# Placing TensorE's side products in the attention layer of a four-layer convolution kernel

## The chip, the core and the metric

The kernel runs on one core of a Trainium2 chip. The metric is the device time of one execution, in microseconds. Three runs of the kernel before took 3672.72, 3662.45 and 3675.35 us; their median is 3672.72 us.

## What is computed

The input x has 4 images of 256 channels and 48 x 48 pixels. Four layers run one after the other, each of the form x = x + layer(group norm of x). The first three are convolutions. The change lies in the fourth, a linear attention over square windows:

```python
q = sigmoid(einsum('bchw,oc->bohw', x, Wq)).reshape(b * h, d, Hh, Ww)
k = sigmoid(einsum('bchw,oc->bohw', x, Wk)).reshape(b * h, d, Hh, Ww)
v = einsum('bchw,oc->bohw', x, Wv).reshape(b * h, d, Hh, Ww)
v = v / maximum(norm(v, axis=1, keepdims=True), 1e-12)
for w in (1, 2, 4):                       # windows of 48, 24 and 12 pixels
    wk = box(integral(k), Hh // w)        # sum of k over the window
    wkv = box(integral(k outer v), Hh // w)
    attn = einsum('bdhw,bdfhw->bfhw', q, wkv)
    norm = einsum('bdhw,bdhw->bhw', q, wk)
    outs.append((attn / (norm[:, None] + 1e-06)).reshape(b, C, Hh, Ww))
return einsum('bchw,oc->bohw', concatenate(outs, axis=1), Wout) + bout
```

There are h = 8 heads of d = 32 channels. All data are float32.

## The kernel before

**Layers 0 to 2** fill the first 1388 us or so. The projections of the first image to q, k and v are begun there too.

**Layer 3** works image by image (b, 4 of them), channel half by channel half (ct, 2 halves of 4 heads) and row block by row block (rb, 6 blocks of 8 rows): 48 *blocks* in this order (`order`, before the main loop). Instead of integral images, the kernel computes for each block the scores q times k against *tiles* of keys (8 rows a by 16 columns c), multiplies them with a 0/1 mask for each of the three windows, and multiplies the masked scores with v. A block has 12, 15 or 18 tiles (`tiles_of`, line 1913), 720 tiles in all. Tiles that the smallest window sees ("near") alternate with those that it does not see ("far" in the code) as long as there are both. For key rows that the largest window sees whole, the middle part of its product comes from a ready sum (`window_state`, `whole`), and only strips of columns need the mask.

**One step of the main loop** (it runs over `stream`, defined at line 2069) issues, for tile n:

- `scores` (line 1763): 4 score products s of 32 rows on TensorE, one for each head, into two PSUM buffers of two heads each (pool ps_s);
- `masked` (line 1781): VectorE multiplies s with the masks of the largest window and, for near tiles, of the middle window, into sm; ScalarE copies s to sm where the tile has only the middle window's part left; GpSimd multiplies sm with the mask that remains;
- the `sums` (line 1890) of tile n - LAG, with LAG = 2: products of sm and v, into three accumulators acc, 4 heads side by side;
- `advance()` (line 237), which lets every *side job* go on.

Every engine runs what it is given in this order (`InOrder`, line 135, keeps the program's order). A product that stands in TensorE's queue before the next scores is therefore paid before them.

**Side jobs** are generators. Each `yield n` puts a job to sleep for n steps. `advance()` counts the step and lets the jobs that are due issue what comes next. The jobs with products on TensorE are:

- `qk` and `v` (lines 338 and 373): the projections of the next image, 2 products of 384 columns or 2 of 256 columns into proj_ps;
- `state` (line 1672): transposes of the keys (keys_ps) and products of keys and v (kv_ps) for the ready sums;
- `norms` (line 1577): the denominators. GpSimd subtracts and multiplies box sums (nhi, nlo, nq) in two halves of channels, and TensorE sums over the channels of each head (norm_ps): 3 products for each half, side by side in the array, each of 384 columns;
- `finish` (line 1960): when a block of the second half ct = 1 is done, VectorE multiplies its sums (stage) with reciprocal denominators (rc), one window at a time (`dve.tensor_mul(stage...)`). Then two output products (mo = 0, 1), each an accumulation of 6 products of 384 columns (out_ps <- o and stage in turn), are added to x and stored. o holds the sums of the first half's heads, which went through HBM.

All these use one PSUM bank (pool ps_m, tag st). `bank(steps)` (line 261) waits until the bank is free, and marks it taken for so many steps. It knows nothing of what TensorE has to do:

```python
def bank(steps):
    nonlocal bank_free
    while step < bank_free:
        yield 1
    bank_free = step + steps
```

`prepare` (line 1927) loads o, the residual res and 8 pieces of rc for a block of the second half, in the middle of this block, and lets GpSimd multiply o with its rc. `take("o")` waits for a free o buffer, of which there is one; `finish` gives it back at its end. There are two buffers each of rc and res.

`until(keys)` (line 252) calls `advance()` until something is made that the main loop needs, without a tile in between: what is pending is then issued in one go. At the end of the kernel `while active: advance()` does the same with what is left.

Of the kernel before, what the change touches and what calls it, by code (L numbers as in the profile page):

```python
# [81 lines left out]

LAG = 2
ATTN_EPS = 1e-6


MROWS = [2 * h + RB - 1 for h in HALVES]
MCOL0 = [max(h, KC) for h in HALVES]
# [6 lines left out]
def window_masks():  # L95

    ki, kj = np.divmod(np.arange(P), KC)
    ms = []  # L100
    for h, nr, m0, ncol in zip(HALVES, MROWS, MCOL0, MCOLS):
        qi = np.arange(nr) - h + 1
# [44 lines left out]
def conv_preact_kernel(  # L147
# [84 lines left out]

    step, bank_free = 0, 0
    made = set()
    active = []

    def advance():

        nonlocal step
        step += 1  # L240
        for entry in list(active):
            if entry[0] <= step:
                wait = next(entry[1], None)
                if wait is None:
                    active.remove(entry)
                else:
                    entry[0] = step + wait
# [12 lines left out]

    def bank(steps):

        nonlocal bank_free
        while step < bank_free:
            yield 1
        bank_free = step + steps


    free = {"xr": 2, "xn": 2, "kt": 2, "sq": 2, "vt": 1, "cs": 1, "o": 1, "rc": 2, "res": 2}

# [17 lines left out]
    class Projection:  # L288
# [49 lines left out]
        def qk(self, g, a, name, mo):  # L338
# [5 lines left out]
            yield from take("kt")  # L344
            yield from bank(1)
            ps = self.ps_tile()[:, 0:NB]
# [26 lines left out]
        def v(self, g, a, c):  # L373
# [11 lines left out]
            vt, ss = self.vs[g]  # L385
            yield from bank(1)
            ps = self.ps_tile()[:, 0:C].rearrange("p (h d) -> p h d", d=D)
# [1095 lines left out]
    with (  # L1483
# [93 lines left out]
        def norms(b, rb):  # L1577
# [51 lines left out]
            yield 1  # L1629
            yield from bank(1)  # L1630
            ps = ps_m.tile([P, 512], F32, tag="st", name="norm_ps")
            for ct in range(NCT):
                for wi in range(NW):
                    pe.matmul(
                        ps[D * wi : D * (wi + 1), 0:NB],
                        head_sel[:, ct, :],
                        sums[ct][:, wi].rearrange("p r w -> p (r w)"),
                        start=(ct == 0),
                        stop=(ct == NCT - 1),
                    )  # L1640
            yield 1
            ns = scr.tile([D * NW, NB], F32, tag="ns", name="ns", bufs=1)
# [29 lines left out]
        def state(b, ct, a):  # L1672
# [3 lines left out]
            yield FETCH  # L1676
            yield from bank(2)
            ps = ps_m.tile([P, 512], F32, tag="st", name="keys_ps")[:, 0 : NKC * P]
# [60 lines left out]
        def rows_whole(a, rb):  # L1739

            return abs(a - rb) * RB + RB <= HALVES[0]
# [10 lines left out]
        class Block:  # L1752
# [28 lines left out]
            def masked(self, a, c, ss):  # L1781
# [145 lines left out]
        def prepare(i):  # L1927
# [32 lines left out]
        def finish(i, stage):  # L1960
# [11 lines left out]
            os = (o, stage)  # L1972
            for wi in range(NW):
                dve.tensor_mul(stage[:, wi], stage[:, wi], rc[:, wi])
                yield 1
            free["rc"] += 1
            for mo in range(NCT):
                yield from bank(2)
# [79 lines left out]
        def done(i):  # L2058
# [13 lines left out]
            for n, (a, c) in enumerate(tiles_of(rb))  # L2072
        ]
        blocks, ahead = {}, []
        start(window_state(0))
        start(finish_all())
        for n in range(len(stream) + LAG):
# [8 lines left out]
            if n >= LAG:  # L2086
# [12 lines left out]
                if last:  # L2099
                    done(i)  # L2100
            advance()
        while active:
# [45 lines left out]
```

## Time and profile before

| what | value |
|---|---|
| median of 3 runs | 3672.72 us |
| time of the profiled execution | 3665.04 us |
| span in its profile | 3663.2 us |
| mean granted TensorE clock | 0.952 |
| first score product of layer 3 | 1388.1 us |
| TensorE busy from 1388 to 3660 us | 2054.9 of 2272 us |
| VectorE busy there | 1494.5 us |
| GpSimd busy there | 1506.5 us |
| ScalarE busy there | 401.1 us |

The span runs from the first to the last instruction. The profile page gives each engine's busy time, a row of 40 slices of the span, the chain of work that ended last, and groups of instructions by operation and tile (out<-in) with the mean time of one and the idle time of the engine before them. A line of the waits view names the engine and operation that waited, what it waited for, the sum, the count and the longest. A line of the timeline has the start, the length, the engine, the operation, the tiles and the count, and in brackets the idle time before it and what ended it. PE is TensorE, PEld its weight load, DVE VectorE, ACT ScalarE, POOL GpSimd, SPq the queue of SyncE that issues DMAs. A product in float32 shows as two records.

### The profile page before, as it was taken

Reading aid. Unit: us, or ns where it says so; the run is one execution under the profiler, and the core shown is the slowest. Engines: PE = TensorE matmul, PEld = TensorE weight load, DVE = VectorE, ACT = ScalarE, POOL = GpSimd, SP = SyncE. Lnnn points to the kernel's source line nnn. Section 1 sums busy time; section 2 is a strip of 40 time slices with the busy share of each in tenths; the row PEclk is TensorE's granted clock in tenths of the full one; section 3 lists DMA queues with packets and bytes.
Section 4 is the critical chain, followed back from the end, with each engine's and each line's share of the span. In section 5 each row is a group of like instructions: output and inputs, shape, how many; then the busy total and the mean of one; then the engine's idle time right before and its main releaser. Section 6 shows DMA issues by size and latency. Waiting matters only on the chain. (4 is left out here: it accounts for less than half of the span.)

```text
span 3663.2 us, 73044 instructions
## 1 busy us (share of the span) xinstructions
PE 3216.3 (88%) x28754; PEld 1942.3 (53%) x28754; DVE 2419.0 (66%) x4987; ACT 677.5 (18%) x1557; POOL 1661.6 (45%) x2548
## 2 busy tenths in 40 slices
PE   3689998998997887887899889899998899999998
PEld 2467686786785664443444444444444444444444
DVE  7976587487484365876756576765577656566664
ACT  0012111111114422222101222211222201111100
POOL 0000120030030034787876786776476777454552
PEclk9789999999998898999999999999999999999999
DMA  7746324324314423344533543344223344211222
GB/s 252 227 139 197 105 94 129 112 85 127 102 65 138 136 72 108 122 141 144 149 103 112 157 122 122 108 126 137 81 96 120 119 128 129 64 32 32 66 62 61
DMA packets 373031, 423.29 MB, mean 116 GB/s; under 512 B 129075, under 2 KB 328531, under 8 KB 371539
## 3 DMA queue, kind: packets, MB, share of 16 engines
q1 hardware_dynamic: 371491, 416.32, 36.9%
q8 instruction: 229, 3.75, 0.4%
q0 software_dynamic: 144, 1.52, 0.2%
q14 instruction: 111, 0.91, 0.1%
q10 hardware_dynamic: 1056, 0.79, 0.1%
HBM read 288.79 MB, written 131.25 MB: 115 GB/s over the span
## 5 line engine op out<-in xcount | busy, mean ns | idle before, releaser
L143 DVE TENSOR_TENSOR sm<-s,masks 128x128 f32<-128x128 f32 (+8 forms) x2592 | 1145.8, 496 | 709.7 <-PE s L143 377.7
L143 POOL TENSOR_TENSOR sm<-sm,masks 128x432 f32<-128x432 f32 (+14 forms) x1152 | 822.9, 728 | 711.3 <-DVE sm L143 512.6
L143 PE MATMUL s<-qs,ks 32*128 32x320 f32 (+3 forms) x5760 | 870.4, 505 | 109.4 <-DVE sm L143 72.5
L143 PE MATMUL acc<-sm,vs 128*32 128x64 f32 (+13 forms) x14976 | 683.0, 308 | 32.2 <-POOL sm L143 32.1
L143 PE MATMUL cv<-vx,wt 128*128 128x288 f32 x2080 | 556.9, 423 | 92.3 <-DVE vx L143 49.5
L143 PEld LDWEIGHTS s<-qs,ks 32*128 32x128 f32 x5760 | 353.1, 188 | 479.8 <-issue 195.8
L143 PEld LDWEIGHTS acc<-sm,vs 128*32 128x32 f32 x14976 | 351.0, 111 | 441.6 <-issue 269.4
L143 PEld LDWEIGHTS cv<-vx,wt 128*128 128x128 f32 x2080 | 400.5, 197 | 212.6 <-issue 55.0
L143 POOL MEMSET v<- 128x16 f32 (+1 forms) x120 | 18.6, 215 | 722.4 <-DVE vx L143 628.3
L143 ACT COPY sm<-s 128x234 f32<-128x234 f32 (+5 forms) x384 | 123.4, 343 | 915.8 <-PE s L143 784.4
L143 PE MATMUL cv<-v,wl 128*128 128x384 f32 x1152 | 224.3, 354 | 22.4 <-DVE x L143 8.6
L143 PEld LDWEIGHTS cv<-v,wl 128*128 128x128 f32 x1152 | 214.6, 195 | 32.2 <-issue 15.2
L143 POOL TENSOR_TENSOR pt<-pt 128x144 f32<-128x144 f32 x336 | 185.3, 552 | 23.4 <-DVE pt L143 0.5
L143 POOL TENSOR_TENSOR v<-l2v,v 128x384 fp32r<-128x384 f32 x96 | 109.0, 1165 | 127.4 <-ACT v L143 118.7
L143 POOL TENSOR_TENSOR nhi<-nhi,nq 128x384 f32<-128x384 f32 x144 | 144.9, 1034 | 0.3
L143 PE MATMUL cv<-pad,wl 128*128 128x384 bf16 x864 | 143.1, 327 | 0.0
L143 PE MATMUL out_ps<-o,wout_sb 128*128 128x384 f32 x288 | 124.2, 514 | 12.3 <-DMA rc<-r_d 7.6
L143 ACT COPY stage<-acc 128x384 f32<-128x384 f32 x144 | 64.0, 489 | 303.7 <-PE acc L143 272.7
L143 PE MATMUL out_ps<-stage,wout_sb 128*128 128x384 f32 x288 | 118.4, 493 | 0.7 <-DVE stage L143 0.7
L143 DVE TENSOR_TENSOR vx<-v 128x868 f32<-128x868 f32 x112 | 115.3, 1055 | 0.5
L143 PEld LDWEIGHTS <-wl 128*128 128x128 bf16 x864 | 83.9, 97 | 59.4 <-issue 0.8
L143 DVE SCALAR_TENSOR_TENSOR x<-cv,alpha,x 128x384 f32<-128x384 f32 x144 | 83.9, 610 | 41.7 <-PE cv L143 41.4
(174 smaller groups left out, 3347.4 us busy)
## 6 DMA issues: line engine op xcount, KB each, us to landing
wt<-wt SPq DMA_DIRECT2D x48, 768.0 KB
kb_d<-pt SPq DMA_DIRECT2D x48, 576.0 KB
rc<-r_d SPq DMA_DIRECT2D x192, 144.0 KB
nhi<-kb_d SPq DMA_DIRECT2D x120, 192.0 KB
nlo<-kb_d SPq DMA_DIRECT2D x88, 192.0 KB
o_d<-stage SPq DMA_DIRECT2D x24, 576.0 KB
o<-o_d SPq DMA_DIRECT2D x24, 576.0 KB
wl<-wl_d SPq DMA_DIRECT2D x16, 768.0 KB
```

Of the source, the lines that this page charges most:

```text
L143: return lambda *args, **kwargs: self.tc.keep_in_program_order(op(*args, **kwargs))
```

## The change

- **An account of room.** `advance` gets a time for the step: 150 ns plus the VectorE time of the tile's masks (`mask_time`) less TensorE's time for the sums of the tile two steps before (`sums_time`), but at least 150 ns. The variable `spare` carries debts from step to step, but no savings. A side product is issued only when `spare` is at least 0.6 of its cost, and the cost is taken off. Costs count 1.67 ns for a column. In `until`, at the end and in the layers before, `advance()` has no time, and room is unlimited.
- **Output products in three pieces** of 2 products each, one for each window, each of which waits for room (`turn`). The bank is held (`HOLD`) until the last piece. In the first output product, the multiplication of stage for a window stands right before its piece, with one step between them; before, the three multiplications came first, a step apart.
- **Norms in two pieces**, one for each half of the channels.
- **Two buffers of o** in place of one, for the sums of the first half's heads. To make space, the mask of the largest window keeps only the rows that are used (23 in place of 55), and `times_mask` picks among them.

The products, the masks' values and what each engine computes stay the same.

```diff
-MROWS = [2 * h + RB - 1 for h in HALVES]
+MROWS = [3 * RB - 1 if h == H // 2 else 2 * h + RB - 1 for h in HALVES]
...
-    def advance():
+    def advance(time=None):
-        nonlocal step
+        nonlocal step, spare
         step += 1
+        spare = ALL if time is None else min(spare, 0.0) + time
...
+    ALL = 1e6
+
+    def turn(cost):
+        nonlocal spare
+        while spare < 0.6 * cost:
+            yield 1
+        spare -= cost
+
-    def bank(steps):
-        nonlocal bank_free
-        while step < bank_free:
+    def bank(steps, cost):
+        nonlocal bank_free, spare
+        while step < bank_free or spare < 0.6 * cost:
             yield 1
         bank_free = step + steps
+        spare -= cost
+
+    def keep_bank(steps):
+        nonlocal bank_free
+        bank_free = step + steps
+
+    def product_time(columns):
+        return 1.67 * columns
...
-    free = {"xr": 2, "xn": 2, "kt": 2, "sq": 2, "vt": 1, "cs": 1, "o": 1, "rc": 2, "res": 2}
+    free = {"xr": 2, "xn": 2, "kt": 2, "sq": 2, "vt": 1, "cs": 1, "o": 2, "rc": 2, "res": 2}
...
-            yield from bank(1)
+            yield from bank(1, NCT * product_time(NB))      # qk; v alike with C
...
-            yield from bank(1)
+            yield from bank(HOLD, 2 * product_time(NB))
             ps = ps_m.tile([P, 512], F32, tag="st", name="norm_ps")
             for ct in range(NCT):
+                if ct > 0:
+                    yield 1
+                    yield from turn(2 * product_time(NB))
...
+            keep_bank(1)
...
-            yield from bank(2)
+            yield from bank(2, product_time(NKC * P))       # keys and kv in state
...
+                    if wi == 0:
+                        mr = RB - 1 if full else 0 if a > rb else 2 * RB - 1
...
-            o = op.tile([P, NW, NB], F32, tag="o", name="o", bufs=1)
+            o = op.tile([P, NW, NB], F32, tag="o", name="o")
...
-            for wi in range(NW):
-                dve.tensor_mul(stage[:, wi], stage[:, wi], rc[:, wi])
-                yield 1
-            free["rc"] += 1
             for mo in range(NCT):
-                yield from bank(2)
+                yield from bank(HOLD, NCT * product_time(NB))
                 ps = ps_m.tile([P, 512], F32, tag="st", name="out_ps")[:, 0:NB]
                 for kt in range(NW * NCT):
+                    if kt % NCT == 0:
+                        if kt > 0:
+                            yield 1
+                            yield from turn(NCT * product_time(NB))
+                        if mo == 0:
+                            wi = kt // NCT
+                            dve.tensor_mul(stage[:, wi], stage[:, wi], rc[:, wi])
+                            yield 1
                     pe.matmul(
...
+                keep_bank(2)
+                if mo == 0:
+                    free["rc"] += 1
...
+        def mask_time(i, a, c):
+            rb = order[i][2]
+            def product(wi, cols):
+                y0, y1 = rows_seen(wi, a, rb)
+                return 2 * (2 * (y1 - y0) * (cols[1] - cols[0]) + 130) / 0.96
+            if not rows_whole(a, rb):
+                return product(0, cols_seen(0, c))
+            time = sum(product(0, cols) for cols in strips(c))
+            if seen(NW - 1, a, rb):
+                return time + product(1, cols_seen(1, c))
+            return time + 300
...
+            time = 1000.0
+            if LAG <= n < len(stream):
+                time = 150.0 + mask_time(*stream[n][:3]) - sums_time(*stream[n - LAG][:4])
+            advance(max(time, 150.0))
```

`sums_time` adds 1.67 ns for each column of the tile's sum products in each window that sees it, 300 ns for the first tile of a block and the time of the ready sums' products in the seventh.

More of the change, by code (lines that the diff above doesn't have):

```diff
@@ L83 @@
 LAG = 2
+HOLD = 1000
 ATTN_EPS = 1e-6
-MROWS = [2 * h + RB - 1 for h in HALVES]
+MROWS = [3 * RB - 1 if h == H // 2 else 2 * h + RB - 1 for h in HALVES]
 MCOL0 = [max(h, KC) for h in HALVES]
@@ L101, in window_masks @@
     for h, nr, m0, ncol in zip(HALVES, MROWS, MCOL0, MCOLS):
-        qi = np.arange(nr) - h + 1
+        qi = np.arange(2 * h + RB - 1)
+        if nr < len(qi):
+            qi = np.r_[qi[: RB - 1], qi[h - 1 : h - 1 + RB], qi[-RB:]]
+        qi = qi - h + 1
         qj = np.arange(ncol) - m0
@@ L228, in conv_preact_kernel @@
     proj = {}
-    step, bank_free = 0, 0
+    step, bank_free, spare = 0, 0, 0.0
     made = set()
     active = []
-    def advance():
-        nonlocal step
+    def advance(time=None):
+        nonlocal step, spare
         step += 1
+        spare = ALL if time is None else min(spare, 0.0) + time
         for entry in list(active):
@@ L385, in v @@
             vt, ss = self.vs[g]
-            yield from bank(1)
+            yield from bank(1, NCT * product_time(C))
             ps = self.ps_tile()[:, 0:C].rearrange("p (h d) -> p h d", d=D)
@@ L1629, in norms @@
             yield 1
-            yield from bank(1)
+            yield from bank(HOLD, 2 * product_time(NB))
             ps = ps_m.tile([P, 512], F32, tag="st", name="norm_ps")
             for ct in range(NCT):
+                if ct > 0:
+                    yield 1
+                    yield from turn(2 * product_time(NB))
                 for wi in range(NW):
@@ L1684, in state @@
             yield 1
-            yield from bank(2)
+            yield from bank(2, product_time(NKC * P))
             ps = ps_m.tile([P, 512], F32, tag="st", name="kv_ps")[:, 0 : NKC * P]
@@ L1972, in finish @@
             os = (o, stage)
-            for wi in range(NW):
-                dve.tensor_mul(stage[:, wi], stage[:, wi], rc[:, wi])
-                yield 1
-            free["rc"] += 1
             for mo in range(NCT):
-                yield from bank(2)
+                yield from bank(HOLD, NCT * product_time(NB))
                 ps = ps_m.tile([P, 512], F32, tag="st", name="out_ps")[:, 0:NB]
                 for kt in range(NW * NCT):
+                    if kt % NCT == 0:
[6 more added lines that the diff above has]
+                            yield 1
                     pe.matmul(
@@ L2073, in conv_preact_kernel, with sums_time @@
         ]
+        def mask_time(i, a, c):
[9 more added lines that the diff above has]
+            return time + 300
+        def sums_time(i, a, c, at):
+            rb, time = order[i][2], 0
+            for wi in range(NW):
+                if seen(wi, a, rb):
+                    y0, y1 = rows_seen(wi, a, rb)
+                    parts = strips(c) if wi == 0 and rows_whole(a, rb) else [cols_seen(wi, c)]
+                    time += product_time((y1 - y0) * sum(p1 - p0 for p0, p1 in parts))
+            if at == 0:
+                time += 300
+            if at == 6:
+                time += product_time(sum(RB * (c1 - c0) for c0, c1 in map(cols_whole, range(NKC))))
+            return time
         blocks, ahead = {}, []
@@ L2100, in conv_preact_kernel @@
                     done(i)
-            advance()
+            time = 1000.0
+            if LAG <= n < len(stream):
+                time = 150.0 + mask_time(*stream[n][:3]) - sums_time(*stream[n - LAG][:4])
+            advance(max(time, 150.0))
         while active:
```

## The prediction

> **What bounds the kernel now.** I read the page first (parts 1, 2, 5), then the waits of the attention stretch (from 1500 us on), then the timeline, step by step.
>
> ```profile
> PE 3216.3 (88%) x28754; PEld 1942.3 (53%) x28754; DVE 2419.0 (66%) x4987; ACT 677.5 (18%) x1557; POOL 1661.6 (45%) x2548
> ...
> L143 PE MATMUL out_ps<-o,wout_sb 128*128 128x384 f32 x288 | 124.2, 514 | 12.3 <-DMA rc<-r_d 7.6
> ```
>
> TensorE looks like the bound, and the change adds no product and removes none. So the first question is whether 88% is real. [...] an out_ps record lasts 514 ns, but in a run of them one starts every 0.325 us. By the busy row, TensorE is free for 2272 - 2055 = 217 us of the attention (window 1388 to 3660 us), and that would cap the gain. By the starts, scores need 405 us, sums 558, side products 415 (384 columns cost 0.64 us): 1380 of 2272 us. I use the second.
>
> ```profile
> DVE sm L143 <- PE s L143: 354.5, 270, 7.7
> ...
> PE s L143 <- DVE sm L143: 67.8, 200, 2.4
> ...
> PEld norm_ps L143 <- POOL nhi L143: 25.8, 32, 3.7
> ```
>
> VectorE waits 354.5 us for scores while TensorE waits for VectorE's masks: the two take turns, neither is full, and what stands between two score products on TensorE's queue lengthens the turn. I call a step what lies from one tile's score products to the next tile's. There are 720, and their lengths come from the starts of the s products in TensorE's timeline. By their masks there are 384 near tiles (mean VectorE mask work 2.2 us by the change's account), 192 mid (1.2) and 144 far (1.6). Most of a block alternates near with mid or far. The longest output group looks like this:
>
> ```profile
> 2483.70 0.91 PE L143 MATMUL out_ps<-o,wout_sb 128*128 128x384 f32 x2
> ...
> 2487.03 0.81 PE L143 MATMUL out_ps<-stage,wout_sb 128*128 128x384 f32 x2
> ...
> 2487.77 0.93 PE L143 MATMUL s<-qs,ks 32*128 32x384 f32 x8
> ...
> 2488.79 2.31 DVE L143 TENSOR_TENSOR sm<-s,masks 128x624 f32<-128x624 f32 x6 [4.67 <-PE s L143]
> ```
>
> Six products hold the queue for 4.07 us; VectorE idles 4.67 us.
>
> **What side work costs by place.** Blocks of one row repeat to 0.01 us, so a step with side work can be compared with the same tile elsewhere without. An output group (3.85 us) in a mid step costs 3.86 us (median of 13, with the step after it), in a far step 3.41 (10), in a near step 3.50 (2): it hides 0.2 us on average. A small product in a near step is different:
>
> ```profile
> 2718.91 2.31 DVE L143 TENSOR_TENSOR sm<-s,masks 128x624 f32<-128x624 f32 x6 [1.01 <-POOL pt L143]
> 2719.73 1.13 PE L143 MATMUL proj_ps<-wv_sb,xn 128*128 128x256 f32 x4
> 2720.79 1.41 PE L143 MATMUL s<-qs,ks 32*128 32x336 f32 x8
> ```
>
> This step lasts 2.90 us and the next 1.85; without the projection the tile has 2.37 and 2.37. A product of 1.06 us is paid wholly out of the wait for masks. Eleven such near steps without a POOL stall hid 1.0, 0.95, 0.8, 0.6, 0.6, 0.5, 0.4, 0.2, 0.2, 0 and -0.2 us (own length, 1.06 us for v and 1.48 for q or k, less what the step and the next grew). I take 0.5 per near piece, with 0.2 and 0.9 as ends.
>
> **Step 1: output products in three pieces.** The order of instructions of both programs shows where they stand. Before, 43 steps hold output groups: 10 near, 15 mid, 18 far. After, 122 steps hold pieces of 1.28 us: 93 near, 12 mid, 17 far. 48 groups x 3 pieces x 0.76 near x 0.5 us = 55 us hidden, against 48 x 0.2 = 10 before: -45 us. At 0.2 per piece it is -12, at 0.9 it is -88. The excess of side time over the change's own room per step gives about the upper end: summed over the 720 steps it falls from 172 to 69 us (-103, for all side work).
> The pieces of the first product now follow their stage multiplication (DVE, 782 ns) by one step instead of up to three. On VectorE's queue masks stand behind it, as before, in single multiplications; TensorE waits for it only if its next scores and sums (0.5 + 0.4 us at least) are shorter than the multiplication and its signal. That is 0 to 0.3 us x 72 pieces, so 0 to 22 us; before, this wait was 0.7 us in all, so I take 3. Two more cuts per group cost about 0.1 us each (the first pair of a run has 0.91 us, a later one 0.81): 48 x 2 x 0.1 = 10 us at most. It is inside the measured piece costs, so nothing is added.
>
> **Step 2: norms in two pieces.** Before, both halves stand a fixed few steps behind their POOL work, and TensorE waits in the middle:
>
> ```profile
> 2101.80 2.89 POOL L143 TENSOR_TENSOR nhi<-nhi,nq 128x384 f32<-128x384 f32 x3
> ...
> 2102.84 2.73 PE L143 MATMUL norm_ps<-nhi,head_sel 128*32 128x384 f32 x6 [1.48 <-POOL nhi L143]
> ```
>
> The first to last starts of the 24 norms sum to 54.3 us, against 24 x 0.98 for unstalled ones: 31 us of stall, mean 1.3, longest 5.6. The second half now stands at least one step (2.3 to 3 us) later, mostly two, so most of it should go: -22 us (ends -10 and -31). What is late next is the sum that waits for POOL's mask (102.1 us of such waits for the weight loads), which the change leaves.
>
> **Step 3: two o buffers.** In mid-kernel the output group merely moves, and nobody waits for o. At the end they do:
>
> ```profile
> 3635.85 0.34 SPq L143 DMA_DIRECT2D o<-o_d  x1
> ...
> 3636.72 5.78 SPq L143 DMA_DIRECT2D rc<-r_d  x8
> ...
> 3644.46 2.89 POOL L143 TENSOR_TENSOR o<-o,rc 128x384 f32<-128x384 f32 x3 [13.33 <-DMA rc<-r_d]
> 3645.51 1.65 PE L143 MATMUL out_ps<-o,wout_sb 128*128 128x384 f32 x2 [7.60 <-DMA rc<-r_d]
> ...
> 3647.82 1.65 PE L143 MATMUL out_ps<-stage,wout_sb 128*128 128x384 f32 x2 [0.67 <-DVE stage L143]
> ```
>
> The last block's o, res and eight rc loads start only when the block before it is finished. With two buffers, o, res and half of the rc loads are issued some 25 us earlier; the other half wait for the third stage multiplication of that block, now about 8 us before the loads of today. Then the last outputs wait for the last sums instead: stage copies end at 3638.5, a multiplication makes it 3639.3, against 3645.5 to 3647.8. That is 6 to 8 us. The pairs after the wait also start 1.28 us apart, not 0.65. [...] Without the gap, six pairs save 0.6 us each by the row, 3.4 us more. By the loads alone I would say -7, with the clock -10. I take -10 (ends -4 and -12). [...] the granted clock over the attention is 0.96 already. I give it nothing.
>
> **Step 4: everything else that waits for room.** Key and kv products gain 28 near steps (21 to 49): 28 x 0.3 = -8 us. Projections lose 11 near steps (65 to 54): 11 x 0.5 = +5. The bank is held for several steps per group, so what needs it comes later. What falls due is flushed: steps with over 2.5 us of side work besides the tail were 43 and are 7, of 3.2 to 5.8 us where the worst was 9.4. Their loads on SP and masks on POOL move with the products by a few steps, and none has a consumer in the same steps: 0. The first layers use the same scheduler but with unlimited room there, and the masks' load shrinks (1.52 MB on the software queue, far ahead of use): 0.
>
> **Sum.** -45 + 3 - 22 - 10 - 8 + 5 = -77 us against the profiled execution's 3665.0 us (span 3663.2): 3588. The median of the three runs is 3672.7, 7.7 above the profiled one, so I lean a little up: 3590 us.
>
> **Rivals.**
> - The room is real for all pieces (chance 0.17). Two adjacent steps with side work overlap: a row of five small ones, 5.6 us together, cost 3.9 (2 of them). Then 0.9 per piece, -88 - 28 - 12 - 10 = -138 us: 3530. Against it: four of the eleven hid 0.2 us or less.
> - The room is mostly not there (0.22). Near steps are themselves one half of the loop scores, masks, scores; three pieces in successive near steps lengthen the same half, and POOL waits (102 us) take what is won. Then -12 - 15 - 8 = -35 us, 3632 us; with the norm stall kept as well, 3650 (no change to speak of).
> - Slower (0.05). TensorE waits at each of the 72 first-product pieces for its stage multiplication, queued behind a whole tile's masks (2.2 us). At 1 us a piece it cancels everything (72 us against 77); at 2.2 us it costs 158, less 77: 3746. For it: one step of distance. Against it: the scores ahead of the piece themselves wait for those masks, so the multiplication is next on VectorE. At 1.5 us a piece: 3700.
> - My forecast, 3565 to 3612 (0.56).
>
> A measurement of this kernel can tell about 0.5% (18 us) from no change. Faster than that 0.86, within it 0.09, slower 0.05. For 8 in 10: 3530 to 3645.
>
> **What would show it.** Right: the idle of 4.67 us before masks gone, DVE's wait for PE s well below 354.5 us; norm stalls (POOL nhi) near zero; no DMA wait before the last out_ps, and full-speed pairs there. The account is wrong if near steps with a 1.28 us piece are longer by 1.28 and the next is no shorter. Step 1 is wrong if a wait of out_ps for DVE stage appears with tens of us. The whole is wrong if DVE or POOL waits for each other grow by what TensorE saves.

## The result, and the profile after

The changed kernel takes 3649.47 us (median of 7 runs, 3640.23 to 3656.03) against 3672.72 us for the kernel before in 7 runs on the same chip: ratio 0.9933, 95% interval 0.9913 to 0.9953. That is 23 us faster, where 77 were forecast; the time lies above the range on record. Its profiled execution took 3656.03 us, with a span of 3654.3 us at a mean granted clock of 0.943 (0.952 in the profile before). Layer 3, from its first score product to the end of TensorE's last product, went from 2270.9 to 2254.2 us in the two profiles. Up to there the order of instructions is the same; the first score product starts at 1388.1 us before and at 1395.8 us after, and anywhere from 1388 to 1403 us in the profiles of all runs, so this difference needn't be the change's.

The page after, with the output products' two groups (busy and mean ns, then the idle time before them):

```profile
PE 3184.0 (87%) x28754; PEld 1921.4 (53%) x28754; DVE 2408.1 (66%) x4987; ACT 677.1 (19%) x1557; POOL 1668.1 (46%) x2548
...
L147 PE MATMUL out_ps<-o,wout_sb 128*128 128x384 f32 x288 | 134.1, 548 | 4.2 <-DVE res L147 3.4
...
L147 PE MATMUL out_ps<-stage,wout_sb 128*128 128x384 f32 x288 | 120.4, 501 | 0.0
```

The idle time before output products fell from 12.3 to 4.2 us, and before those that read stage it is 0.0. So the slower outcome that I feared for the one step between multiplication and product didn't come. The waits of the attention stretch (from 1500 us on; sum, count, longest), after and then two lines of before:

```profile
DVE sm L147 <- PE s L147: 285.3, 240, 10.4
...
DVE sm L147 <- POOL sm L147: 137.1, 122, 6.6
...
PE s L147 <- DVE sm L147: 51.7, 147, 2.9
...
PE acc L147 <- POOL sm L147: 48.2, 44, 4.9
DVE sm L147 <- POOL nhi L147: 32.0, 20, 4.0
ACT xn L147 <- DMA xr<-x_d: 27.9, 3, 14.4
...
DVE sm L147 <- POOL o L147: 21.6, 13, 3.2
```

```profile
DVE sm L143 <- POOL sm L143: 96.9, 92, 4.8
...
PE acc L143 <- POOL sm L143: 32.1, 39, 5.2
```

Two things are to be seen. VectorE waits 69 us less for scores (354.5 before), and no line "norm_ps <- POOL nhi" is left: as forecast. But TensorE's sums wait 48.2 us for GpSimd's masks (32.1 before), VectorE waits 32.0 and 21.6 us for GpSimd's nhi and o (22.1 and 11.2 before), and ScalarE 27.9 us for loads (3.9 before). Those lines are where to look for what is missing; waits overlap, so their sums can't simply be added. The last sign of being wrong that I had named came too: VectorE's waits for GpSimd (sm, nhi and o) grew by 60 us together, while its wait for scores fell by 69. But two thirds of this growth are the line for sm, and in runs 6 and 7 below that line grows by 52 us (78.1 to 129.7) although there the gain is kept; so it alone doesn't show a loss.

Where no other side job disturbs, the pieces look as I drew them. Timeline of block 2 in the second half of image 3 (b = 3, ct = 1), a piece in a near step and the next one:

```profile
3490.44 0.91 PE L147 MATMUL out_ps<-o,wout_sb 128*128 128x384 f32 x2
...
3491.19 0.81 PE L147 MATMUL out_ps<-stage,wout_sb 128*128 128x384 f32 x2
3491.93 0.82 PE L147 MATMUL s<-qs,ks 32*128 32x320 f32 x8
3492.68 0.57 PE L147 MATMUL acc<-sm,vs 128*32 128x84 f32 x16
3492.84 0.81 DVE L147 TENSOR_TENSOR sm<-s,masks 128x256 f32<-128x256 f32 x2 [1.46 <-issue]
```

VectorE idles 1.46 us where a whole output group made it idle 4.67. Image 3 has no projections and no norms in its second half, so its blocks compare directly (us for a block, two output groups in each):

| block of (3, ct = 1) | before | after | change |
|---|---|---|---|
| 1 | 42.8 | 41.8 | -1.0 |
| 2 | 49.4 | 47.3 | -2.1 |
| 3 | 49.5 | 47.0 | -2.4 |
| 4 | 43.3 | 42.4 | -0.9 |

The mean is -1.6; scaled to the 24 blocks of the second halves that is -39 us, against my -45. This is an estimate from four blocks, since no run has the pieces alone. The tail after:

```profile
3599.06 1.97 SPq L147 DMA_DIRECT2D o<-o_d  x1
...
3641.07 0.88 PE L147 MATMUL out_ps<-o,wout_sb 128*128 128x384 f32 x2 [0.76 <-issue]
...
3641.78 0.81 PE L147 MATMUL out_ps<-stage,wout_sb 128*128 128x384 f32 x2
```

The last o is loaded 42 us before its use, no DMA ends a wait, and the pairs start 0.65 us apart at a granted clock of 1.00 (3641 to 3650 us). Before, the clock was 0.50 from 3645.5 to 3652 us, where the pairs started 1.28 us apart; the share of the clock in my -10 was an estimate from these distances. The last step shrank from 28.9 to 17.8 us: -11, against my -10.

So steps 1 and 3 of the forecast came, by this estimate about 50 us of them, and something gave 27 back. By halves of images (90 steps each), the second halves, which hold most output pieces, are 54 us shorter in sum, the first halves, with most projections, 37 us longer.

### The profile page after: what moved, and what is told of

Its sections match the earlier page's. It is cut to its first block, busy times and chain, and to the rows that moved or that the text cites. A ratio compares the mean times of both kernels' runs of the same rounds, so it can differ in the third digit from the quotient of the medians.

```text
span 3654.3 us, 73033 instructions
## 1 busy us (share of the span) xinstructions
PE 3184.0 (87%) x28754; PEld 1921.4 (53%) x28754; DVE 2408.1 (66%) x4987; ACT 677.1 (19%) x1557; POOL 1668.1 (46%) x2548
## 5 line engine op out<-in xcount | busy, mean ns | idle before, releaser
L147 PE MATMUL s<-qs,ks 32*128 32x320 f32 (+3 forms) x5760 | 819.4, 511 | 109.0 <-DVE sm L147 55.8
L147 PE MATMUL acc<-sm,vs 128*32 128x64 f32 (+13 forms) x14976 | 689.9, 310 | 49.0 <-POOL sm L147 48.2
L147 PEld LDWEIGHTS s<-qs,ks 32*128 32x128 f32 x5760 | 329.5, 190 | 487.7 <-issue 204.5
L147 PE MATMUL out_ps<-o,wout_sb 128*128 128x384 f32 x288 | 134.1, 548 | 4.2 <-DVE res L147 3.4
L147 PE MATMUL proj_ps<-xn,wk_sb 128*128 128x384 f32 x192 | 89.8, 596 | 31.3 <-ACT sg L147 24.6
```

Source lines behind the costliest of these rows:

```text
L147: return lambda *args, **kwargs: self.tc.keep_in_program_order(op(*args, **kwargs))
```

## The experiments

Eighteen kernels ran, numbered in their order; each was timed beside runs of the kernel before on its chip. A time below is a median, with its ratio to the kernel before and the 95% interval; a difference in us is a difference of such ratios times 3672.7. Three theories were on record for the first eight: **A**, long waits for GpSimd, made by side jobs that now fall together, ate the gain; **B**, near steps have no room; **C**, the tail is the whole gain. **N** (the divided norm holds the bank too long) and **S** (SP's queue) came later.

**Is the forecast gain there at all? Runs 6 and 7.** GpSimd's work for norms, key sums and o is left out of both kernels:

```diff
-                        pool.tensor_sub(hi[:, wi, n:RB], hi[:, wi, n:RB], lo[:, wi, n:RB])
+                        pass
...
-                    pool.tensor_mul(hi[:, wi], hi[:, wi], qf)
...
-                    pool.tensor_add(pt[:, :, r, :], pt[:, :, r, :], up)
...
-            pool.tensor_copy(carry[:, mo], pt[:, :, RB - 1, :])
...
-                pool.tensor_mul(o[:, wi], o[:, wi], rcs[0][:, wi])
```

> The changed kernel without the GpSimd work of norms, key sums and o (the subtractions, additions and multiplications of nhi, pt, carry and o are left out, so denominators and output products get wrong values; masks, squares and ready sums stay on GpSimd). TensorE's order stays that of the changed kernel. To be set against the same cut of the kernel before, e7. Theory A (GpSimd stalls ate the gain): e6 is 45 to 70 us faster than e7 (pieces and placing 35 to 45, tail about 10). Theory B (near steps hide little): 10 to 20 us faster, the tail and no more.

> The kernel before with the same GpSimd work left out (nhi, pt, carry and o; denominators and output products get wrong values). Long stalls behind GpSimd and the 31 us in the norms go: 3560 to 3610 us by theory A, whose weight rests on these stalls; 3630 us or more if they matter little.

Changed: 3532.50 us, 0.9626 (0.9596 to 0.9656). Before: 3593.38 us, 0.9790 (0.9762 to 0.9818). The change is worth 60 us here, within A's answer (45 to 70), so B and C fall. The waits, first of run 7 (before), then of run 6 (changed), from 1390 us on:

```profile
DVE sm L143 <- PE s L143: 374.6, 289, 7.1
```

```profile
DVE sm L147 <- PE s L147: 263.1, 258, 7.1
```

The wait that the pieces are to shorten fell by 111 us, and no product of the sums waits for a mask on GpSimd in either (their weight loads wait 0.5 us at most). GpSimd's side work costs the changed kernel 36 us (+-17) more than the kernel before. A stood, and its picture is this one, after the change (image 3, first half, block 0):

```profile
3159.14 2.92 POOL L147 TENSOR_TENSOR nhi<-nhi,nlo 128x384 f32<-128x384 f32 x3
...
3162.02 1.00 POOL L147 TENSOR_TENSOR o<-o,rc 128x384 f32<-128x384 f32 x1
...
3162.97 2.90 POOL L147 TENSOR_TENSOR nhi<-nhi,nq 128x384 f32<-128x384 f32 x3
3165.82 1.00 POOL L147 TENSOR_TENSOR o<-o,rc 128x384 f32<-128x384 f32 x1
3166.77 2.53 POOL L147 TENSOR_TENSOR sm<-sm,masks 128x168 f32<-128x168 f32 x4
...
3167.34 1.18 PE L147 MATMUL acc<-sm,vs 128*32 128x84 f32 x14 [4.85 <-POOL sm L147]
```

Eight side operations, in four groups, keep GpSimd busy until it gets to one tile's masks, and TensorE waits 4.85 us. This step takes 8.62 us; in the kernel before, where nothing stands in it, it takes 1.98.

**Which step of mine brings that? Runs 10, 14, 16 and 13: the norms.** Run 10 puts the norm products of the changed kernel together again:

```diff
             for ct in range(NCT):
-                if ct > 0:
-                    yield 1
-                    yield from turn(2 * product_time(NB))
                 for wi in range(NW):
```

> The changed kernel with each norm product in one piece again, its account and everything else kept. By my forecast's step 2 the split is worth 22 us: 3671. Theory A (the wait for GpSimd's norm operations only moves, from the norm's second half to the sums behind the same operations): 3645 to 3655, no more than 6 us either way. If the split itself costs (two turns to wait for, the bank held longer): 3630 to 3643.

3618.96 us, 0.9874 (0.9852 to 0.9897): 22 us (11 to 33) less than the changed kernel, and the fastest of the kernels that do the whole work. My step 2, forecast at -22, costs about as much. A, which said no more than 6 us either way, missed; nearer was the answer that the split itself costs. The waits of run 10, from 1500 us on:

```profile
PE acc L147 <- POOL sm L147: 24.1, 32, 4.7
PEld norm_ps L147 <- POOL nhi L147: 20.5, 21, 4.2
...
PE norm_ps L147 <- POOL nhi L147: 5.0, 2, 3.5
```

The stall inside the norms is back, nearly as large as before (25.8 and 4.7), but the wait of the sums has halved, from 48.2 to 24.1. These two changes are of one size, so the moved stall explains why nothing was won by step 2, not why it cost 22 us. A second thing stands in the steps: at the starts of images 2 and 3, the steps of 11.39 and 11.74 us, in which TensorE waits for late ready sums, take 3.15 us each, and the flushes of 12 output records six steps before them are flushes of 8.

Run 14 does step 2 alone in the kernel before:

```diff
-            yield from bank(1)
+            yield from bank(1000)
...
             for ct in range(NCT):
+                if ct > 0:
+                    yield 1
...
+            keep_bank(1)
             yield 1
```

> The kernel before with step 2 alone: norm products in two pieces one turn apart, the bank held between them, no account. My forecast's step 2: 22 us less than the kernel before (10 to 31 less). Theory N: the bank is used by all side jobs here too, but there is no account to wait for and an output group holds it for one turn, so sliding costs less: 5 to 20 us more. Theory A: the stall moves to the sums: within 5 us.

3677.64 us, 1.0018 (1.0005 to 1.0032): 7 us slower (2 to 12), at the border between A's answer (within 5 us) and N's (5 to 20 more). One place shows how the stall moves. Before, image 2, second half (timeline):

```profile
2966.93 2.93 POOL L143 TENSOR_TENSOR nhi<-nhi,nq 128x384 f32<-128x384 f32 x3
...
2967.40 3.34 PE L143 MATMUL norm_ps<-nhi,head_sel 128*32 128x384 f32 x10
...
2969.79 1.51 POOL L143 TENSOR_TENSOR sm<-sm,masks 128x312 f32<-128x312 f32 x2
```

The same tiles in run 14:

```profile
2973.29 2.92 POOL L143 TENSOR_TENSOR nhi<-nhi,nq 128x384 f32<-128x384 f32 x3
...
2976.17 1.00 POOL L143 TENSOR_TENSOR o<-o,rc 128x384 f32<-128x384 f32 x1
...
2977.12 2.83 POOL L143 TENSOR_TENSOR sm<-sm,masks 128x352 f32<-128x352 f32 x4
2978.04 1.33 PE L143 MATMUL acc<-sm,vs 128*32 128x176 f32 x6 [1.84 <-POOL sm L143]
```

Before, TensorE spends GpSimd's multiplications inside the norm (3.34 us for 10 records), and the masks behind them are ready when the queue goes on. In run 14 the norm no longer waits; the scores and sums of the next tile go first, and these wait for masks that stand behind the same multiplications and one of o. The three steps take 10.35 us before and 12.70 in run 14. Over the stretch (from 1500 us on), the sums' wait for GpSimd grew from the 32.1 us shown above while the norm's own 30.5 went:

```profile
PE acc L143 <- POOL sm L143: 48.4, 56, 6.0
```

That is 16 us more against 30 less, and still the time rose. VectorE's wait for scores grew from 354.5 to 388.1 us in the same stretch; how much of the loss that is, no run separates.

Run 10 charges the whole norm to the account like one half of it. Run 16 is run 10 with the whole norm charged in full (4 instead of 2 times `product_time(NB)`), run 13 is run 10 without GpSimd's side work.

> The tenth run, but the whole norm is charged to the account in full (2565 ns by its own rule, not 1283). It tells whether the tenth run gained by the undivided norm or by the smaller room that it asked for. If by the undivided norm (Theory N): within 6 us of the tenth run, ratio 0.986 to 0.989. If by the smaller charge: back at the changed kernel's 0.992 to 0.995, since a norm then waits for a far or mid step and holds up the queue.

> The changed kernel with norm products in one piece and, as in the sixth run, without GpSimd's work for norms, key sums and o (that part of the computation is left out). Against the sixth run (ratio 0.9626, 3532.5 us), which has the norms in two pieces. Theory N (a split norm holds the bank for one or two turns more, so all that queues for the bank slides, whatever GpSimd does): about 20 us less, 3505 to 3520 us, 0.956 to 0.959 of the kernel before. Theory A (the split costs only by GpSimd's crowd, which the second half falls into): no difference, 3526 to 3540. If the split is good once GpSimd is free (there is no stall left for it to remove, so this speaks for finer pieces alone): over 3540.

Run 16: 3638.17 us, 0.9903 (0.9882 to 0.9924), between the two answers: half of run 10's 22 us came with the undivided norm, half with the smaller room that it asked for, each known to 11 us only, so that either could be near nothing. Run 13: 3528.41 us, 0.9608 (0.9590 to 0.9626), 7 us (+-13) under run 6. As a total this is within A's answer (no difference) and below N's (20 us). But the places show that N holds where image 1, 2 or 3 starts. From 1390 us on, TensorE waits for ready sums (wide) in run 6, with GpSimd's side work out:

```profile
PE acc L147 <- POOL wide L147: 9.5, 3, 3.7
```

The steps at the starts of images 2 and 3 take 11.15 and 10.43 us there, almost as in the changed kernel, and 3.15 us in run 13, as in run 10; the wait is 2.0 us in run 13. In run 6 and in the changed kernel both halves of a norm stand between the keys' products and the kv products for that ready sum, and kv comes two steps later than in runs 10 and 13, where the norm came before. The first blocks of images 1, 2 and 3 are together 25 us shorter in run 13 than in run 6, and 38 us shorter in run 10 (22 in run 16) than in the changed kernel. Run 13 gives most of this back elsewhere, 17 us in one block (image 1, first half, block 2); run 10 loses as much in the same block, in the step of 17.0 us shown below under SP's queue. So the divided norm costs in two ways: its stall moves to the sums (A), and it holds the one bank longer, so that ready sums come late (N).

**Is it the crowd as such? Runs 4, 9 and 15.** GpSimd's side work is spread, at most two norm operations, one multiplication of o or half a key sum per step:

```diff
+    def pool_slots(steps):
+        nonlocal pool_free
+        while step < pool_free:
+            yield 1
+        pool_free = step + steps
...
+                        if ops % 2 == 0:
+                            yield from pool_slots(1)
+                        ops += 1
                         pool.tensor_sub(hi[:, wi, n:RB], hi[:, wi, n:RB], lo[:, wi, n:RB])
...
             for wi in range(NW):
+                yield from pool_slots(1)
                 pool.tensor_mul(o[:, wi], o[:, wi], rcs[0][:, wi])
```

> The changed kernel with the GpSimd work of norms, key sums and o spread: at most two norm operations, one o multiplication or half a key sum per step, never two jobs in one step. Theory A: the long stalls (54 steps over 1.5 us longer than their own work explains, 187 us together) fall by 30 to 60 us, and some is lost to more flushes (7 and 8 flushed steps): 3610 to 3635 us. Theories B and C: no gain, 3649 us or slower by the later norms.

> The kernel before, with the spreading of GpSimd's side work of the fourth run alone (two norm operations, one o multiplication or half a key sum per step). Theory A (the change crowds GpSimd, and the spreading repairs that): little to repair here, 3660 to 3673 us, at most 12 us under the kernel before, against 12.7 under the changed one. If the spreading is a gain of its own that has nothing to do with the change: at least the same 13 us and probably more, since GpSimd's side work costs 71 us here: 3640 to 3655. If norms and kv sums come late by it: over 3675.

> The tenth run (norms in one piece) with the spreading of GpSimd's side work as well. Alone against the kernel before, norms in one piece within the change gave 46 us and the spreading within the change 39 (24 without the change). If the two are different causes: 10 to 15 us under the tenth run, ratio 0.983 to 0.985, about 3605 us. If the spreading only repaired what the split norms hurt: no more than the tenth run, 0.987. If the spreading makes norms late and they then stand whole in the way: over 0.990.

In the changed kernel (run 4) 3636.80 us, 0.9895 (0.9873 to 0.9917), 14 us less, at the edge of A's answer (3610 to 3635); the sums' wait fell from 48.2 to 26.4 us. In the kernel before (run 9) 3641.58 us, 0.9935 (0.9917 to 0.9953): 24 us, as much as the whole change. So spreading is a gain of its own, and A's claim that it mainly mends the change was wrong. On run 10 (run 15) it adds nothing: 3633.05 us, 0.9882 (0.9864 to 0.9899), within the interval of run 10, although the sums' wait fell further, from 24.1 to 13.2 us. Spreading and undivided norms seem to relieve the same steps; a sum of waits doesn't tell the time.

**The account. Runs 3, 11, 5, 8 and 12.** Run 3 sets `spare = ALL` in every step, so that pieces go one per turn wherever they fall; run 11 does that with the spreading.

> The changed kernel with room always unlimited: pieces a step apart, bank held, two o, but no product waits for room. Near steps get 214 us of side work by the order, against 243 with the account and 156 before. If the account itself is what pays, it is slower than the changed kernel by 0.5 us for each of some 30 pieces, 15 us: 3665 us. If the account costs (it delays keys, kv and projections, so that ready sums come late and jobs bunch), theory A: 3630 to 3645 us. Theory B: no difference, 3649 us.

> The fourth run (changed kernel with GpSimd's side work spread) with the account of room switched off, so that pieces go one per turn wherever they fall. The account alone was worth 23 us without spreading (3672.6 against 3649.5). If the account's worth is in TensorE's room: the same 23 us here, 3655 to 3665. If most of its worth was that it happened to keep jobs with GpSimd work apart: 3636 to 3646.

Run 3: 3672.56 us, 0.9993 (0.9982 to 1.0004). Run 11: 3647.75 us, 0.9949 (0.9932 to 0.9966). Without the account the change gains nothing that can be measured. The account is worth 22 us, with spreading 20 (+-10), which is near the first answer for run 11 (23 us). VectorE's wait for scores (from 1500 us on) is 364.1 us in run 3, where the changed kernel has 285.3, and 373.8 in run 11, where run 4 has 315.7. Both speak for TensorE's room and against B; that the account also keeps jobs on GpSimd apart isn't excluded, since run 11's median, 3647.75 us, lies between its two answers.

Runs 5 and 8 exempt keys and kv from the account (run 8 with the spreading), run 12 lets no output group take the bank while a key or kv product waits (with the spreading):

```diff
-        while step < bank_free or spare < 0.6 * cost:
+        while step < bank_free or (cost and spare < 0.6 * cost):
...
-            yield from bank(2, product_time(NKC * P))
+            yield from bank(2, 0)
```

> The changed kernel with keys and kv products exempt from the account: they wait for the bank alone. If room delays the ready sums and that costs the stalls of 7 us in (2,0,0) and (3,0,0): 3630 to 3642 us. If the bank held by the output pieces delays them, or GpSimd's queue: 3645 to 3652 us, no change against the changed kernel.

> The version with spread GpSimd work (e4) and keys and kv products exempt from the account. If both causes are separate and add up: 3620 to 3630 us. If the keys were never held up by room: as e4, 3637 us.

> The fourth run with one rule more: an output group does not take the bank while a key or kv product of the next state is waiting for it. If the late ready sums at the start of images 2 and 3 (steps of 11.4 and 11.7 us, against 5.4 and 3.9 before) come from the bank that output pieces hold, about 12 us are won: 3620 to 3628. If they are late for another reason (the spread or the account itself): 3633 to 3640. If output groups then come so late that they are flushed: over 3645.

I thought that ready sums are late because keys wait for room or for the bank. Run 5: 3698.19 us, 1.0082 (1.0053 to 1.0111); run 8: 3680.30, 1.0037 (1.0025 to 1.0048); run 12: 3656.18, 0.9971 (0.9961 to 0.9981), all slower than what they changed (the changed kernel for run 5, run 4 for the others), by 28 to 55 us. In run 12 the cause is plain: two flushes of 24.9 and 31.1 us with 20 output records, a whole norm, keys and kv at once. In run 5 the sums' wait for GpSimd grew from 48.2 to 63.0 us; why earlier keys do that I can't say.

**The o buffers. Runs 1 and 2.** Run 1 gives the changed kernel one buffer again (`"o": 1`, `bufs=1`), run 2 gives the kernel before two, and the smaller mask that makes room for them.

> The changed kernel with one o buffer instead of two; account of room and pieces stay. Theory A (long GpSimd stalls, made by jobs that now fall together, ate the gain of the pieces): the tail loses its 11 us again, but the o multiplications no longer fall on the norms' GpSimd work in blocks (1,0,0) and (3,0,0) (two stalls of 6 us): 3648 to 3656 us. Theory C (the tail is the whole gain, all else nets to nothing): 3660 to 3664 us. Theory B (near steps have no room, pieces hide little) says nothing of o: 3660 us.

> The kernel before with two o buffers (and the shorter mask that makes space) alone; no account, no pieces. Tail shorter by 11 to 13 us: 3660 us by all theories if nothing else moves. Its order no longer has the four steps with 4.5 to 9.4 us of flushed products, which cost about their length as single groups too: no gain from that by theory B, up to 5 us by the others. Theory C: the same as the changed kernel, 3650 us; theory A: 3655 to 3662 us.

Run 1: 3738.61 us, 1.0175 (1.0148 to 1.0202), 89 us slower than the changed kernel and far from every answer on record: the pieces make `finish` so long that it is held up by its one buffer and flushed, in nine steps of 11.6 to 21.0 us, and the last step takes 33.5 us. Run 2: 3686.89 us, 1.0040 (1.0024 to 1.0055), slower than before by 15 us, where every answer was a gain, although its tail shrank from 28.9 to 12.8 us. The multiplications of o moved to other steps, and VectorE's wait for nhi on GpSimd went from 22.1 to 39.9 us; that this is the cause isn't shown.

**SP's queue. Runs 17 and 18.** Run 10 still has a step of 17.0 us. Its timeline (SPq is SP's queue of DMA issues):

```profile
2121.33 0.43 SPq L147 DMA_DIRECT2D nq<-q_d  x1
2122.10 0.37 SPq L147 DMA_DIRECT2D nhi<-kb_d  x1
...
2130.76 0.52 SPq L147 DMA_DIRECT2D nlo<-kb_d  x1
2131.38 0.38 SPq L147 DMA_DIRECT2D q_d<-sg  x1
...
2134.59 1.28 ACT L147 ACT_TABLE_LOAD   x1 [10.92 <-DMA q_d<-sg]
...
2136.43 2.93 PE L147 MATMUL proj_ps<-xn,wq_sb 128*128 128x384 f32 x4 [12.04 <-ACT sg L147]
```

A projection's store stands behind a norm's loads for 10 us; ScalarE waits for the store, the projection for ScalarE, and the scores stand behind it. Run 13, without GpSimd's side work, has the same step (17.1 us). Both runs spread these loads over six turns:

```diff
                         sync.dma_start(
                             out=lo[:, wi, n:RB], in_=kb_d[b][wi, chans, y0 + n : y0 + RB, :]
                         )
-                return hi, lo, qf
+                    yield 1
+                loaded.append((hi, lo, qf))
...
-            yield FETCH
+            yield FETCH - 1
```

> The changed kernel with the loads of a norm (up to 20, issued in one turn on SP's queue) spread over six turns, one window of one half at a time. Theory S (projections that now come one per step have their stores and loads behind these on SP, ScalarE waits for them and TensorE for ScalarE: 42.7 us of TensorE waits for ScalarE's sg in the changed kernel, 24.1 before): 8 to 18 us less than the changed kernel, 3632 to 3641 us, ratio 0.9885 to 0.991. If SP's queue is only where the profile happens to show late work: within 6 us, 0.992 to 0.995. If norms come late by six turns and end in a flush: over 0.996.

> The tenth run (norms in one piece, 0.9874) with the same spread loads. Its longest step, 17.0 us at 2122 us, was TensorE waiting 12.0 us for ScalarE, which waited 10.9 us for a store of projections behind some 16 norm loads on SP. Theory S: 8 to 18 us less, 3600 to 3611 us, ratio 0.982 to 0.985. If not SP: 0.986 to 0.989. If late norms cost: over 0.990.

Run 17: 3692.57 us, 1.0062 (1.0040 to 1.0083); run 18: 3646.57 us, 0.9932 (0.9910 to 0.9955): 47 and 21 us slower. The waits of run 18, from 1390 us on:

```profile
PE acc L147 <- POOL sm L147: 37.0, 49, 3.8
...
PEld norm_ps L147 <- POOL nhi L147: 33.6, 35, 3.4
PE proj_ps L147 <- ACT sg L147: 27.4, 20, 4.3
```

The wait that I aimed at fell from 40.7 to 27.4 us in run 18 (in run 17 it rose, from 29.0 to 34.9); the two for GpSimd rose from 24.1 and 20.5 by 13 each. As a way to gain, S falls. SP's queue does make stalls of 10 us; that norms a few turns later meet other jobs on GpSimd is what these lines suggest, not more.

## Why the prediction was wrong

| step | forecast, us | measured, us | from |
|---|---|---|---|
| 1, output products in three pieces | -45 + 3 | -39, estimated | four undisturbed blocks |
| 2, norms in two pieces | -22 | +22 or +11 in the change (each +-11), +7 alone | runs 10, 16, 14 |
| 3, two o buffers | -10 | -11 at the tail | last step |
| 4, everything else | -3 | +5 to +16 | what is left of -23 |

**Step 2 failed, and it is the larger part of the miss.** "The second half now stands at least one step (2.3 to 3 us) later, mostly two, so most of it should go": the stall inside the norm did go, to the last us. I also wrote what is late next, "the sum that waits for POOL's mask", and then gave it nothing, as something "which the change leaves". The timeline of run 14 shows this sum waiting behind the very operations the norm had waited for, and the waits of runs 14 and 10 agree. GpSimd took its work in the program's order there (nhi at 2973.29 us, o at 2976.17, the masks at 2977.12); before, while TensorE stood in the norm (3.34 us), GpSimd caught up, and the stall wasn't lost on top of the later wait but took its place. That makes the gain nothing. The cost comes in part from what step 4 says of the bank, "what needs it comes later", and gives no price: the divided norm holds the bank, kv comes two steps later, and TensorE waits for ready sums, also with GpSimd's side work out (25 us between runs 6 and 13 at the starts of three images). Between -22 and the measured +11 to +22 lie 33 to 44 of the 54 us that are missing.

**Step 4 failed at its zero.** "Their loads on SP and masks on POOL move with the products by a few steps, and none has a consumer in the same steps: 0." The consumer isn't that of the moved operation but of the tile mask queued behind it. With GpSimd's side work taken away the change is worth 60 us, and 67 (0.9608 against 0.9790) with norms undivided; with it 25 (by the ratio) and 46. The difference, 36 (+-17) and 21 us (+-15), is what the change loses to GpSimd's side work. Forecast without step 2, 55 us, stands beside 46 in run 10 and 36 in run 16.

**The clock was put at nothing too.** Of the clock outside the tail I wrote "the granted clock over the attention is 0.96 already", and "I give it nothing". The clock records of the two traces, before and after, hold two values, 1.0 and 0.5. In layer 3 the stretches at 0.5 sum to 163 us before and 221 us after, and TensorE is busy for 142.5 and 184.5 us of them. The mean clock agrees over all runs: its median is 0.952 in 140 runs of the kernel before and 0.945 in the seven of the changed one. At full rate that work would take about half as long (the same six products take 1.35 us at a clock of 1.0 and 2.50 at 0.5, shown at the end), so up to 21 us of the miss, by this estimate, went through the clock; they are part of what steps 2 and 4 lost, not more on top. It isn't the pieces as such: with GpSimd's side work out the change lowers the half-rate time, from 118 us in run 7 to 85 in run 6.

**Steps 1 and 3 held,** by mechanism and, as far as the undisturbed blocks and the tail tell, by size: 0.87 of the piece gain, no wait for stage, the tail to 1 us, full-speed pairs. That the account measures room is supported by run 3. For the buffers one correction: in the kernel before they alone cost 15 us (run 2), in the changed one they are needed (run 1), so the tail is only what is easy to see of them.

**The rivals.** "The room is mostly not there", with the norm stall kept 3650, has the right number and the wrong reason: the room is there, and "POOL waits (102 us) take what is won" was its true half. I should have given that half a price of its own. The slower case, waits for stage, didn't happen.

**What stays open.** Steps 1 to 4 don't add up edit by edit: earlier keys, a keys-first rule and spread loads each moved the time by 20 to 55 us against their reasons, probably because each shifts what meets on GpSimd and on the bank. How the 5 to 16 us of step 4 divide between GpSimd, the ready sums, the clock and SP wasn't settled.

## What to carry to other kernels

A stall that ends at another engine's queue needn't go when TensorE goes on (in run 14 the norm's 30.5 us went and 16 came at the sums): ask what the next instruction waits for, and if it stands behind the same work on that engine, count nothing. A job cut in pieces holds its buffer for longer: price what waits for that buffer. When side jobs are moved, list their instructions on every engine and look at what is queued behind them, not only at who reads them. A test kernel with one engine's side work left out tells in one run how much of a gain is lost to meetings there.

## What the runs showed of the hardware

The granted clock of 0.5 that stands at the tail before appears in mid-kernel too. After the change, at the late ready sums of image 3 (timeline):

```profile
3181.26 2.50 PE L147 MATMUL acc<-qs,wide 128*128 128x192 f32 x6 [3.58 <-POOL wide L147]
...
3185.76 1.51 PE L147 MATMUL out_ps<-o,wout_sb 128*128 128x384 f32 x2
```

Of the 48 groups of six such products in this trace, 44 take 1.35 us each, at a granted clock of 1.0; three take 2.50, at 0.5, this one among them, after 3.58 us of idle time. An output pair takes 0.81 to 0.91 us at 1.0 and 1.51 here, most of it at 0.5: the granted clock is 0.50 from 3181 to 3187 us and 1.00 from 3187 to 3192. So with this wait came slower products behind it, 1.15 us for the six and 0.60 to 0.70 for the pair, on top of its own length.

The stretches at one clock, 112 in the record before and 138 after, all last a multiple of 3.41 us, but for the last of each. Cut into such steps, layer 3 of both profiles has 44 steps at a clock of 1.0 in which TensorE was busy for less than half, and 41 of them were followed by 0.5; of 1040 in which it was busy for 80% or more, 5 were. Most of these falls follow no long wait: before 30 of the 39 falls after the change, no gap of TensorE that reached into the step ahead was as long as a step. What sets the clock the traces don't show.
